# A graph layer on one core: rewritten edge rows and separate own messages against all edges as they lie

## The chip, the cores and the metric

The kernel runs on one core of one Trainium2 chip. The metric is the device time of one execution in microseconds (us), the median of several executions. A run of ten executions of the kernel before gave a median of 17,891.4 us (17,885.6 to 17,897.53).

A core has five engines that each run their own queue of instructions: TensorE (PE, with its weight loads listed as PEld), VectorE (DVE), ScalarE (ACT), GpSimd (POOL) and SyncE (SP). In this kernel SP issues the plain DMAs, and POOL issues the indirect DMAs, that is, the gathers of rows by index.

## The reference

There are 50,000 nodes with 160 numbers each (64 scalars and 32 vectors of 3), and 1,650,000 directed edges with 4 numbers each. The edges come sorted by their target, and every node has one edge to itself among them.

```python
    _loop = jnp.arange(50000, dtype=jnp.int32)
    src = jnp.concatenate([_s, _d, _loop])
    dst = jnp.concatenate([_d, _s, _loop])
    _o = jnp.argsort(dst, stable=True)
...
        m = jnp.concatenate([out0, out1.reshape(-1, 3 * MUL1)], axis=1)
        m_agg = jax.ops.segment_sum(m, dst, num_segments=n)
...
        return x + jax.nn.relu(h)
...
    x = _layernorm(x + _L0_gnn_ref(...), axis=-1)
```

The message `m` of an edge is linear in the source's row `x[src]` and in the edge's four numbers, so the sum over edges can be taken first, of row times edge number, and the weights applied afterwards to each node's sum. Then come a second linear map, relu, the residual and a layer norm. The output is 50,000 x 160 in float32.

## The kernel before

**Groups.** 128 edges make a unit, 6 units (`G`) make a group of 768 edges. A group's targets lie within 32 neighbouring nodes (`W`). For each unit POOL gathers 128 rows of `x` with one indirect DMA (`gather`, L370): 128 rows of 640 B. DVE builds a matrix that has an edge's four numbers in the columns of its target (`spread`, L379 `hot`, L382 `ha`). PE multiplies the two (`group_sums`, L407), six units summed in PSUM. DVE transposes the result (`turn_sums`, L419) and adds it into a ring in SBUF, at a place that is read from a register (L428).

**Tiles.** Two groups (`PG = 2`, a "pair") share one tile of gathered rows `xg`, of 12 gathers. There are 4 buffers of `xg` (pool `rows`), and 2 of the PSUM tile `ps`. The loop at L893 writes out the order by hand for SP, PE, DVE and ACT: in pair p, PE's products run; behind the first of them DVE turns the sums of pair p-1; behind the third, DVE spreads pair p+1. POOL's queue isn't part of that written order and holds nearly nothing but gathers. A gather waits for the landing of an earlier gather that used the same semaphore (there are eight, 110 to 117), and the first gather of a pair also waits for PE's semaphore (118), for the last reader of the buffer it overwrites.

**Supersteps.** 20 groups (`SG`) are loaded and placed at once (`load`, `cast`, `place`, L253 to L364).

**Blocks.** When no later group can touch 128 neighbouring nodes, these are a block: 10 products (`block`, L728, 5 matmuls in two passes), then relu, residual and norm (`norm1` to `norm3`, L184 to L198), one block at a time, and one output DMA for two blocks. All this is handed out between the gathers' products by `after_pair` and `work`.

**Rewritten rows.** After the first 100 groups (`HEAD`), edges are not taken as they lie. `pack` (L486 to L650) reads 790 edges into each of 128 partitions, finds the edges that go from a node to itself, closes the gaps with predicated copies (L582 to L591), and SP writes each row to DRAM (`edges`) at an address from a register (`store`, `put`, L640). The numbers of the removed edges go to `selves`. Supersteps after the first 100 groups load from `edges`. So the removed edges are not gathered.

**Own messages.** The removed edges' part is added densely: for two blocks at once SP reads the nodes' rows four times and their numbers once (`ask_own`, L700 and L705), DVE multiplies (L711 to L713) and transposes them into the ring (L717), in place of part of the zeroing at L675 (`set_own`, `begin_segment`).

This leaves 2,087 groups, that is 12,522 gathers. At the end a flag decides whether a slow second pass (L957 on) is needed.

Of the kernel before, what the change touches and what calls it, by code (L numbers as in the profile page):

```python
# [67 lines left out]
PG = 2  # L68
SG = 20

HEAD = 100
BP = 2
SB = 4
RP = 128
RS = 16
KM = 31
REST = 15
LEAD = 3

def plan(n_nodes, n_edges):  # L80

    nblk = 125
    assert n_nodes % nblk == 0
    assert W == FB
    nb = n_nodes // nblk
    again = 9

    per_unit = P * n_nodes / n_edges
    group = max(g for g in range(1, 17)
                if g == 1 or (g + 0.2) * per_unit + 1 + 5 * math.sqrt(g * per_unit * per_unit / P) <= W)  # L90
    head = math.ceil(min(HEAD, n_edges / (group * P)) / SG) * SG
    eh = head * group * P
    row = group * P + math.floor(per_unit * group * (1 - n_nodes / n_edges))
    assert row * n_nodes / n_edges + 5 * math.sqrt(row * n_nodes / n_edges / 16) < KM

    far = math.ceil(6 * math.sqrt(n_edges) / 2 * n_nodes / n_edges) + 2
    rows = math.ceil((n_edges - eh) / row) + 2
    ngroups = math.ceil((n_edges - n_nodes + eh * n_nodes / n_edges + far) / (group * P))
    assert eh + (rows - 1) * row - n_nodes + eh * n_nodes / n_edges - far >= ngroups * group * P
    units = P * math.ceil(max(math.ceil(n_edges / P) + again - 1, math.ceil((eh + rows * row + 1) / P)) / P)  # L100
    return nblk, nb, again, group, units, ngroups, row, head, rows, far
# [3 lines left out]
def tile_gnn_resnorm(ctx: ExitStack, tc: tile.TileContext, x, src, dst, attr, W1, W2, W3, W4, W5, Ws, Wv, out, n_edges):  # L105
    nc = tc.nc
    N = x.shape[0]
    NBLK, NB, GA, G, NU, NG, L, NH, NR, FAR = plan(N, n_edges)
    EH = NH * G * P
# [71 lines left out]
    def norm1(pool, ph, xt, n):  # L181

        y = pool.tile([P, D], F32, name="y")
        nc.vector.scalar_tensor_tensor(y[:n], ph, 0.0, xt, op0=ALU.max, op1=ALU.add)  # L184
        st = pool.tile([P, 6], F32, name="st")
        nc.vector.bn_stats(st[:n], y[:n])  # L186
        mv = pool.tile([P, 2], F32, name="mv")
        nc.vector.bn_aggr(mv[:n], st[:n])  # L188
        return y, mv

    def norm2(pool, mv, n):
        rstd = pool.tile([P, 1], F32, name="rstd")
        nc.scalar.activation(rstd[:n], mv[:n, 1:2], AF.Sqrt, bias=eps_t[:n])  # L193
        return rstd

    def norm3(o, y, mv, rstd, n):
        nc.vector.reciprocal(rstd[:n], rstd[:n])
        nc.vector.tensor_scalar(o[:n], y[:n], mv[:n, 0:1], rstd[:n], op0=ALU.subtract, op1=ALU.mult)  # L198
        return o
# [4 lines left out]
    def near(g):  # L204
        p = g * G * P
        return p / degree if p <= EH else EH / degree + (p - EH) / (degree - 1)

    nblocks = math.ceil(N / P)
    S = SB * P
    cuts = sorted({0, NH, NG} | {round(i * NG / 10 / SG) * SG for i in range(10)})  # L210
    parts = list(zip(cuts, cuts[1:]))
    offs = []
    for g0, g1 in parts:
        t = min((near(g) / N for g in range(g0, g1 + 1)), key=lambda t: abs(t - 0.5))
        offs.append(math.ceil(5 * math.sqrt(n_edges * max(0, t * (1 - t))) / (degree - 1) + 10))
# [13 lines left out]
    with tc.tile_pool(name="once", bufs=1) as once, tc.tile_pool(name="raw", bufs=2) as rawp, \  # L229
            tc.tile_pool(name="idx", bufs=2) as idxp, tc.tile_pool(name="rows", bufs=4) as rowp, \  # L230
            tc.tile_pool(name="ops", bufs=3) as op, tc.tile_pool(name="sums", bufs=3) as sump, \
            tc.tile_pool(name="ring", bufs=2) as ringp, tc.tile_pool(name="node", bufs=3) as np_, \
            tc.tile_pool(name="ahead", bufs=4) as aheadp, tc.tile_pool(name="outs", bufs=3) as outp, \
            tc.tile_pool(name="psC", bufs=1, space=PSUM) as psC, tc.tile_pool(name="psK", bufs=2, space=PSUM) as psK, \
            tc.tile_pool(name="psP", bufs=1, space=PSUM) as psP, tc.tile_pool(name="psA", bufs=2, space=PSUM) as psA, \
            tc.tile_pool(name="psM", bufs=2, space=PSUM) as psM, ExitStack() as later_pools:

        spotp, ownp = (later_pools.enter_context(tc.tile_pool(name=name, bufs=bufs))
                       for name, bufs in (("spot", 3), ("own", 2)))
# [8 lines left out]
        shareP, sumP = bank[:, 3, 64:64 + NK], bank[:, 3, 96:96 + BP * P // W]  # L248
# [4 lines left out]
        def load(s):  # L253
# [3 lines left out]
            u0, f0 = (g0 * G, g0) if s + 1 < NSC else ((g0 + ng) * G - P, g0 + ng - W)  # L257
# [13 lines left out]
            if g0 >= NH:  # L271
                C = 2 + NK
                if s * SG > NH:
                    f0 = g0 + ng - W
                    at = (at[0], g0 - f0, ng)
                p0, q0 = u0 * P - EH, f0 * G * P - EH
                r6 = rawp.tile([P, NK, W, C], F32, name="r6")
                fd = rawp.tile([P, 1], F32, name="fd")
                fetch_first(fd, edges[0, q0 * C + 1:(q0 + W * G * P) * C + 1], C)
                fetch(r6.rearrange("p b e c -> p b (e c)"), edges[0, p0 * C:(p0 + P * P) * C], C)  # L280
                return s, at, None, None, fd, r6[:, :, :, 0:2].rearrange("p b e c -> p c b e"), r6[:, :, :, 2:]
# [8 lines left out]
            return s, at, ri, fi, None, None, ra  # L290

        def cast(loaded):
            s, at, ri, fi, fd, ef, af = loaded
            if ri is not None:
                ef = rawp.tile([P, 2, NK, W], F32, name="rf")
                fd = rawp.tile([P, 1], F32, name="ff")
                nc.scalar.copy(fd, fi)
                begun.append(nc.scalar.copy(ef, ri))
            return s, at, fd, ef, af
# [23 lines left out]
        def find(g):  # L323

            if g not in spot_of:
                s, u = g // SG, g % SG
                n = min(SG // 2, NG - g)
# [67 lines left out]
        def wrote(kind, ins):  # L395
            ws = written[kind]
            for old in ws[-3] if len(ws) > 2 else []:
                tc.declare_no_dep(ins.ins, old, reason="its reader has waited for it")
# [31 lines left out]
        halves = ((0, L // 2), (L // 2, L))  # L430
        C = 2 + NK
        npacks = math.ceil(NR / RP)
        real = math.ceil((n_edges - EH) / L)
        LW = math.ceil(L / W) * W

        def row_start(r):

            lo, hi = (math.floor(r * L * (1 - 1 / degree)) - 2 * FAR - 2, math.ceil(r * L * (1 - 1 / degree)) + 2 * FAR + 2)
            return (max(lo, 0), hi if r else 0), (max(math.floor((EH + r * L) / degree) - FAR - 2, 0),
                                                  math.ceil((EH + r * L) / degree) + FAR + 2)  # L440

        edges = dram.tile([1, (row_start(NR - 1)[0][1] + L) * C], F32, name="edges")
        selves = dram.tile([1, (row_start(NR - 1)[1][1] + W) * NK], F32, name="selves")
        edge_bytes = edges.bitcast(U8).rearrange("o f -> (o f)")
        self_bytes = selves.bitcast(U8).rearrange("o f -> (o f)")
        rows_stored = [0]

        def row_table(tmp):

            NT = npacks * RP  # L450
            raw = tmp.tile([1, NT], I32, name="raw")
            at = tmp.tile([1, NT], F32, name="at")
            node = tmp.tile([1, NT], F32, name="node")
            nc.vector.memset(raw[:, NR:], 0)
            with nc.allow_non_contiguous_dma(reason="one number of each row"):
                dq.dma_start(raw[:, :NR], dst[EH:EH + NR * L].rearrange("(o r e) -> o r e", o=1, e=L)[:, :, 0])

            nz = math.ceil((row_start(0)[1][1] + W) / P)
            zeros = tmp.tile([P, nz * NK], F32, name="zeros")
            nc.vector.memset(zeros, 0.0)  # L460
            dq.dma_start(selves[0, 0:P * nz * NK].rearrange("(p f) -> p f", p=P), zeros)
            nc.gpsimd.iota(at, pattern=[[L, NT]], base=0, channel_multiplier=0, allow_small_or_imprecise_dtypes=True)
            most, least = math.ceil(EH / degree) + FAR, max(math.floor(EH / degree) - FAR, 0)
            nc.vector.tensor_scalar(node, raw, float(N), float(-most), op0=ALU.min, op1=ALU.add)
            nc.vector.scalar_tensor_tensor(node, at, 1 / degree, node, op0=ALU.mult, op1=ALU.min)
            nc.vector.tensor_scalar(node, node, float(most - least), None, op0=ALU.add)
            nc.vector.scalar_tensor_tensor(node, at, 1 / degree, node, op0=ALU.mult, op1=ALU.max)
            nc.vector.tensor_scalar(node, node, float(least), None, op0=ALU.add)

            nc.vector.tensor_copy(spots[:, :NT], node)  # L470
            nc.vector.tensor_copy(node, spots[:, :NT])

            nc.vector.scalar_tensor_tensor(at, at, node[:, 0:1], node, op0=ALU.add, op1=ALU.subtract)

            moved = raw.bitcast(F32)
            nc.vector.scalar_tensor_tensor(moved[:, :NR], raw[:, :NR], float(N), node[:, :NR],
# [9 lines left out]
        def pack(c, follow):  # L486
# [77 lines left out]
            def close():  # L564
# [5 lines left out]
                if f:  # L570
                    nc.vector.tensor_copy(counts[:f, 1, c:c + 1], cum[:f, L:L + 1])
# [526 lines left out]
```

## Time and profile before

| What | Value |
|---|---|
| median of ten executions | 17,891.4 us |
| the profiled execution: its own time | 17,902.41 us |
| the profiled execution: its span | 17,900.7 us |
| gathers, first and last start | 12,522, 12.1 us and 17,869.0 us |
| PE products of groups (L407) | 25,044, 6,572.0 us |
| DVE `ha` (L382), `hot` (L379) | 1,044 each, 1,830.4 and 572.4 us |
| SP DMAs at L640 (row stores) | 4,236, the last at 16,740.7 us |
| mean granted clock of TensorE | 0.62 |

The span is from the first to the last instruction of one profiled execution. Busy times don't add up to it, because engines work side by side. In the groups, "idle before" is the time in which an engine did nothing just before such an instruction, with what ended it. Lines are lines of the kernel before.

### The profile page before, as it was taken

How to read it: one execution, taken by the hardware profiler on the slowest of the kernel's cores; microseconds unless marked ns; L12 is line 12 of the kernel's file. 1: busy time of each engine (PE TensorE's matmuls, PEld its weight loads, DVE VectorE, ACT ScalarE, POOL GpSimd, SP SyncE). 2: the span in 40 equal slices, each digit the busy share in tenths (PEclk: the TensorE clock that was granted, in tenths of full speed). 3: DMA queues.
4: the chain of work that ended last, by engine and by line, in shares of the span. 5: the costliest groups of instructions: out<-in, count | busy, mean ns of one | idle time of the engine just before them, and what ended most of it. 6: DMA issues, size and time to landing. Idle time of an engine off the chain costs nothing.

```text
span 17900.7 us, 99696 instructions
## 1 busy us (share of the span) xinstructions
PE 7069.9 (39%) x28971; PEld 6135.2 (34%) x28972; DVE 7269.6 (41%) x12244; ACT 226.6 (1%) x484; POOL 11883.8 (66%) x12535
## 2 busy tenths in 40 slices
PE   3334334334343333333434334343334433344334
PEld 3333333333333333333333333333333333333333
DVE  5343534335353342534435244343444434334333
ACT  0000000000000000000000000000000000000000
POOL 6666666666666666666666666666666666666666
PEclk6666666666666666666666666666666666666666
DMA  2222232222222222232222222222222222222222
GB/s 77 74 77 75 77 79 69 79 73 77 77 70 79 75 77 77 70 81 72 78 75 75 77 73 78 74 77 75 72 79 75 77 77 70 77 74 71 75 73 61
DMA packets 862904, 1342.39 MB, mean 75 GB/s; under 512 B 272883, under 2 KB 629752, under 8 KB 858364
## 3 DMA queue, kind: packets, MB, share of 16 engines
q0 software_dynamic: 601056, 1026.60, 21.9%
q1 hardware_dynamic: 259856, 308.09, 6.4%
q8 instruction: 231, 3.78, 0.1%
q14 instruction: 321, 2.63, 0.0%
q10 hardware_dynamic: 1440, 1.29, 0.0%
HBM read 1263.67 MB, written 71.40 MB: 75 GB/s over the span
## 4 chain that ended last, share of the span: by engine, by line
issue 35%; POOL 32%; PE 15%; another core or an unknown queue 6%; DMA 3%; DVE 1%; DVEq 0%; POOLq 0%
POOL xg L370 32%; PE ps L407 13%; DMA xg<-in_x,si 3%; PE phb L728 1%; DVE ha L382 0%; DVE ring L428 0%; DVE pra L589 0%; DVE sums L419 0%; DVE hot L379 0%; DVE ring L717 0%; DVEq L328 0%; DVE pri L584 0%; DVE marks L582 0%; DVE hit L586 0%
## 5 line engine op out<-in xcount | busy, mean ns | idle before, releaser
L370 POOL DMA_INDIRECT xg<-in_x,si x12522 | 11880.1, 949 | 5985.5 <-issue 3660.5
L407 PE MATMUL ps<-xg,ha 128*128 128x160 f32 x25044 | 6572.0, 395 | 10446.5 <-issue 9403.9
L407 PEld LDWEIGHTS ps<-xg,ha 128*128 128x128 f32 x25044 | 5433.8, 263 | 11370.8 <-issue 10385.4
L419 DVE STREAM_TRANSPOSE sums<-ps 128x320 f32<-128x320 f32 x1044 | 527.3, 505 | 5217.3 <-remote 3011.5
L184 DVE SCALAR_TENSOR_TENSOR y<-phb,xt 128x160 f32<-128x160 f32 x391 | 125.9, 322 | 4802.8 <-PE ps L407 3116.3
L382 DVE TENSOR_TENSOR ha<-hot,pk 128x1536 f32<-128x1536 f32 x1044 | 1830.4, 1753 | 39.2 <-DVE hot L379 2.1
L728 PE MATMUL phb<-BWk,ring 128*128 128x160 f32 (+1 forms) x3910 | 1174.7, 388 | 323.6 <-issue 323.2
L728 PEld LDWEIGHTS phb<-BWk,ring 128*128 128x128 f32 (+1 forms) x3910 | 928.9, 267 | 331.6 <-issue 330.9
L428 DVE TENSOR_TENSOR ring<-ring,sums 128x160 f32 x2087 | 684.6, 328 | 295.6 <-issue 205.2
L379 DVE TENSOR_TENSOR hot<-bank,rel 128x384 f32<-128x384 f32 x1044 | 572.4, 548 | 0.0
L717 DVE STREAM_TRANSPOSE ring<-xr 128x1280 f32<-128x1280 f32 x188 | 465.2, 2475 | 6.5
L589 DVE COPY_PREDICATED prow<-marks,prow 128x2370 f32<-128x2370 int32 (+8 forms) x160 | 445.7, 2786 | 1.1
L193 ACT ACTIVATE rstd<-mv,eps_t 128x1 f32<-128x1 f32 x391 | 115.2, 295 | 17255.3 <-DVE mv L188 5659.4
L589 DVE COPY_PREDICATED pra<-marks,pra 128x1580 f32<-128x1580 int32 (+8 forms) x160 | 305.8, 1911 | 0.0
L713 DVE TENSOR_TENSOR xr<-xr,bank 128x1280 f32<-128x1280 f32 x188 | 278.9, 1483 | 6.7 <-issue 0.4
L198 DVE TENSOR_SCALAR o<-y,mv,rstd 128x160 f32<-128x160 f32 x391 | 148.1, 379 | 21.2 <-remote 5.0
L425 DVE TENSOR_TENSOR ring<-ring 128x196 f32<-128x196 f32 (+20 forms) x485 | 149.2, 373 | 1.8
L186 DVE BATCH_NORM_STATS2 st<-y 128x6 f32<-128x160 f32 x391 | 128.2, 328 | 13.4
L675 DVE MEMSET ring<- 128x1280 f32 (+1 forms) x98 | 119.3, 1218 | 22.9 <-issue 22.9
L586 DVE COPY_PREDICATED_SCALAR hit<-marks,none 128x395 int32 (+8 forms) x160 | 105.2, 657 | 5.7
L352 DVE STREAM_TRANSPOSE pk<-r 128x512 f32<-128x512 f32 x100 | 104.5, 1045 | 0.0
L587 DVE COPY_PREDICATED hit<-marks,pri 128x395 int32<-128x395 int32 (+8 forms) x160 | 95.6, 598 | 6.2 <-issue 0.7
(343 smaller groups left out, 1681.2 us busy)
## 6 DMA issues: line engine op xcount, KB each, us to landing
xg<-in_x,si POOLq DMA_INDIRECT x12522
xr<-in_x SPq DMA_DIRECT2D x748, 160.0 KB
r<-edges SPq DMA_DIRECT2D x100, 384.0 KB
edges<-prow SPq DMA_DIRECT2D x1994, 18.5 KB
selves<-mine SPq DMA_DIRECT2D x1992, 0.5 KB
xt<-in_x SPq DMA_DIRECT2D x195, 160.0 KB
out<-o SPq DMA_DIRECT2D x195, 160.0 KB
pra<-in_attr SPq DMA_DIRECT2D x15, 1580.0 KB
```

Source lines behind the costliest of these rows:

```text
L198: nc.vector.tensor_scalar(o[:n], y[:n], mv[:n, 0:1], rstd[:n], op0=ALU.subtract, op1=ALU.mult)
L370: nc.gpsimd.indirect_dma_start(out=xg[:, j, :], out_offset=None, in_=x, in_offset=bass.IndirectOffsetOnAxis(ap=placed[0][:, u + j:u + j + ...
L379: nc.vector.tensor_tensor(hot[:, :n], slotsP[:, 0:W].unsqueeze(1).to_broadcast([P, n, W]), rel[:, u:u + n].unsqueeze(2).to_broadcast([P, n ...
L382: nc.vector.tensor_tensor(ha[:, :n], hot[:, :n].unsqueeze(2).to_broadcast([P, n, NK, W]), pk[:, :, u:u + n].rearrange("p k u -> p u k").un ...
L407: mm = nc.tensor.matmul(ps[:, j // G, :], ha[:, j].rearrange("p k w -> p (k w)"), xr, start=j % G == 0, stop=j % G == G - 1)
L419: nc.vector.transpose(at[:, :ng], ps[:, :ng].rearrange("p g (b f) -> p g b f", f=FB))
L425: nc.vector.tensor_tensor(ring[k][:, b, :past], ring[k][:, b, :past], ring[k - 1][:, b, S:S + past], op=ALU.add)
L428: nc.vector.tensor_tensor(here, here, at[:, i], op=ALU.add)
L589: nc.vector.copy_predicated(what[:n, a:e], mi[:, r].unsqueeze(2).to_broadcast([n, e - a, what.shape[2]]), what[:n, a + d:e + d])
L713: nc.vector.tensor_tensor(xr[:, :nq], xr[:, :nq], sumP[:, :nq].unsqueeze(2).to_broadcast([P, nq, D]), op=ALU.mult)
L717: nc.vector.transpose(ring[k][:, :, c0:c0 + nq * W].rearrange("p b (w q) -> p q b w", q=nq), xr[:, :nq].rearrange("p q (b f) -> p q b f", ...
L728: wrote("misc", nc.tensor.matmul(ph[:nb], ring[k][:, i, c0:c0 + nb], BWk[:, i, :], start=i == 0, stop=i == ND - 1))
```

## The change

All edges are taken from the inputs as they lie. `pack`, its DRAM tables, `row_table`, `store` and the checks that belong to them go. `ask_own` and `set_own` go, and the ring is zeroed in full. An edge from a node to itself is gathered like any other. The number of groups becomes `ceil(1,650,000 / 768) = 2,149`, which is 12,894 gathers.

Three groups share a tile (`PG = 3`: 18 gathers to a tile) and a superstep has 21 groups. The pools change: 5 buffers of `xg` in place of 4, 3 of `ps` in place of 2, 2 of `sums` in place of 3, 3 of `xt` in place of 4, 2 of `o` in place of 3. The norms of two blocks share their instructions where the operation allows it. The delays of the handed-out work are cut, in tiles, since a tile is longer.

```diff
-PG = 2
-SG = 20
-HEAD = 100
+PG = 3
+SG = 21
...
-LEAD = 3
+LEAD = 2
...
+    ngroups = math.ceil(n_edges / (group * P))
...
-            tc.tile_pool(name="idx", bufs=2) as idxp, tc.tile_pool(name="rows", bufs=4) as rowp, \
-            tc.tile_pool(name="ops", bufs=3) as op, tc.tile_pool(name="sums", bufs=3) as sump, \
+            tc.tile_pool(name="idx", bufs=2) as idxp, tc.tile_pool(name="rows", bufs=5) as rowp, \
+            tc.tile_pool(name="ops", bufs=3) as op, tc.tile_pool(name="sums", bufs=2) as sump, \
...
-            tc.tile_pool(name="psP", bufs=1, space=PSUM) as psP, tc.tile_pool(name="psA", bufs=2, space=PSUM) as psA, \
+            tc.tile_pool(name="psA", bufs=3, space=PSUM) as psA, \
...
-            if g0 >= NH:
...
-                fetch(r6.rearrange("p b e c -> p b (e c)"), edges[0, p0 * C:(p0 + P * P) * C], C)
...
             ring[k] = ringp.tile([P, ND, TW], F32, name="ring")
-            own = own_blocks(k)
-            end = min((own[-1][-1] + 1) * P, nblocks * P) - k * S if own else 0
-            nc.vector.memset(ring[k][:, :, end:], 0.0)
+            for b in range(ND):
+                nc.vector.memset(ring[k][:, b], 0.0)
...
+            if b == bs[-1]:
+                resid[b] = norm1(np_, sums_of.pop(bs[0])[:nb, :m], of_nodes.pop(bs[0])[:nb, :m], nb, m)
...
-            after_pair(max(p - 3, START), begin_segment, k)
-            for bs in own_blocks(k):
-                got = []
-                for part in range(NK):
-                    after_pair(p - 8 + part, ask_own, k, bs, got, part)
-                after_pair(p - 2, set_own, k, bs, got)
+            after_pair(max(p - 2, START), begin_segment, k)
...
-            for d, f in ((2, do_block), (3, do_root), (4, do_store), (6, do_send)):
+            for d, f in ((1, do_block), (2, do_root), (3, do_store), (4, do_send)):
                 after_pair(p + d, f, b)
...
-                if packs and p >= START:
-                    when = p + (j + 1) / (ng * G)
...
-                    for step in packs[0][done:todo]:
```

## The prediction

> **What bounds the kernel now.** I read the page's busy times and its chain of what ended last, then POOL's waits, then POOL's timeline across a few stalls, then tables of windows cut exactly from one stall's end to the next.
>
> ```profile
> span 17900.7 us, 99696 instructions
> PE 7069.9 (39%) x28971; PEld 6135.2 (34%) x28972; DVE 7269.6 (41%) x12244; ACT 226.6 (1%) x484; POOL 11883.8 (66%) x12535
> issue 35%; POOL 32%; PE 15%; another core or an unknown queue 6%; DMA 3%; DVE 1%; DVEq 0%; POOLq 0%
> ```
>
> No engine is full. POOL is the busiest with 66%, and the chain runs mostly through its gathers and the "issue" time between them.
>
> ```profile
> POOL xg L370 <- issue: 3660.5, 11946, 2.7
> POOL xg L370 <- PE ps L407: 1537.4, 289, 12.0
> POOL xg L370 <- remote: 686.0, 175, 7.0
> POOL xg L370 <- PE phb L728: 59.4, 11, 6.6
> ```
>
> POOL's waits (total us, times, longest): a gather takes 0.95 us and 0.30 us of "issue" lie before the next; and 289 + 175 + 11 = 475 times POOL stands still, 2,282.8 us in all, 4.81 us each.
>
> ```profile
> 17243.87 0.95 POOL L370 DMA_INDIRECT xg<-in_x,si  x1 [0.30 <-issue]
> 17245.12 0.94 POOL L370 DMA_INDIRECT xg<-in_x,si  x1 [0.30 <-issue]
> 17252.30 0.94 POOL L370 DMA_INDIRECT xg<-in_x,si  x1 [6.24 <-PE ps L407]
> 17253.55 0.98 POOL L370 DMA_INDIRECT xg<-in_x,si  x1 [0.31 <-issue]
> ```
>
> In POOL's timeline a gather starts every 1.25 us until a tile's first gather waits some 6 us for PE's semaphore. One would say that PE is late, and that more buffers help. The windows say otherwise. Each begins where a stall ends; columns are PE, PEld, DVE, ACT and POOL busy with instruction counts.
>
> ```profile
> 16945.80:16977.60 31.80, 12.25 (x61) 11.03 (x60) 7.47 (x14) 0.30 (x1) 22.68 (x24) 0.66 0.23 62
> 16977.60:16996.80 19.20, 6.84 (x20) 5.60 (x21) 3.83 (x8) 0.00 (x0) 11.35 (x12) 0.50 0.25 68
> 17098.90:17150.10 51.20, 20.21 (x84) 17.57 (x83) 16.36 (x42) 0.29 (x1) 34.04 (x36) 0.63 0.22 58
> 17150.10:17201.20 51.10, 21.54 (x92) 18.41 (x91) 11.80 (x23) 0.59 (x2) 34.30 (x36) 0.60 0.31 79
> 17252.20:17286.60 34.40, 14.27 (x64) 13.44 (x62) 20.27 (x40) 0.29 (x1) 22.77 (x24) 0.65 0.45 107
> ```
>
> 36 gathers take 51.1 to 51.2 us, whether DVE runs 42 instructions or 23 and PE 84 products or 92: 1.42 us each. 24 gathers take 34.4 us: 1.43 each, with a stall that is shorter in proportion. And where a stall ended early (24 gathers in 31.8), the next took what was missing (12 in 19.2): together 36 in 51.0. Something with a fixed pace of 1.42 us for a gather stands behind POOL; POOL runs ahead of it at 1.25 until the buffers are full, then waits for it. The trace doesn't name it. It isn't PE's count of products or DVE's work, by these rows.
>
> ```profile
> 236.70:698.90 462.20, 182.98 (x743) 160.68 (x742) 202.91 (x323) 4.23 (x16) 306.53 (x324) 0.62 0.26 72
> 877.10:16210.40 15333.30, 6076.27 (x24856) 5277.37 (x24856) 6286.25 (x10512) 191.65 (x405) 10191.67 (x10752) 0.62 0.29 76
> 17098.90:17832.30 733.40, 286.80 (x1195) 245.04 (x1194) 225.98 (x453) 4.71 (x16) 489.40 (x516) 0.61 0.26 68
> ```
>
> Three long windows give the pace with different neighbours. At 236.7 to 698.9, edges come as they lie (the first 600 gathers), `pack` works, and there are no own messages (the first `xr` load is at 728.4): 462.2 / 324 = 1.4265. In the long middle there is everything: 15,333.3 / 10,752 = 1.4261. After the last row store (16,740.7) `pack` is over and own messages go on: 733.4 / 516 = 1.4213.
>
> **The change part by part.** *More gathers.* 2,149 groups in place of 2,087: 12,894 gathers, 372 more. At POOL's own 1.25 us they cost 465 us, at the pace of 1.42 us 529 us.
>
> *`pack` goes.* Its DVE instructions (L448 to L613) sum to 1,946 us and its 4,236 row stores fill SP's queue. All of it lies beside the gathers: with it the pace is 1.4261, without it 1.4213. So it is worth 0.0048 us a gather, 61 us.
>
> *Own messages go, and loads come from the inputs.* DVE's L690 to L720 sum to 831 us, SP's `xr` and `sa` loads are 943 DMAs; a superstep now has four loads and two small ACT casts. The pace with own messages and rewritten rows (1.4261) and without either (1.4265) is the same, so I take nothing. Bounds: half of DVE's remaining load may be worth another 0.0048 (pace 1.4165), or the gain without `pack` may not show (1.4261).
>
> *Zeroing the ring, spreads, norms.* All on DVE, none on the path. A full zeroing is 3.26 us (the 128x3840 form of L675) x 98 = 319 us, against 119 now. `ha` took 1.75 us for 1,536 columns and 0.95 for 768, so 0.15 + 1.046 per thousand columns: 2.56 us for 2,304, x 717 tiles = 1,833, as now (1,830). Joined norms save at most half of their 539 us. DVE ends near 7,270 - 1,946 - 831 + 200 = 4,700 us, a quarter of the span. What covers it is the gap between its tiles, 25.6 us for 18 gathers; if that cover went, 2.6 us a tile x 717 = 1,860 us would be the price, but nothing brings it near.
>
> *What waits now.* A tile's first gather still waits for PE's last reader, five tiles back; behind it in POOL's queue stand only gathers. PE's first product of a tile waits for DVE's `ha`, written one tile ahead, and for a `ps` buffer, of which there are three. SP loses nearly all its queue, so loads and outputs aren't late. Deeper buffers (90 gathers against 48) let POOL run further ahead and stall less often and longer; by the windows that changes no pace.
>
> *Ends.* The first 600 gathers took 877.1 us, 21.4 more than 600 x 1.4261; I keep that (bounds 0, since part of it falls at the first own messages, and 21.4). The last gather started 31.7 us before the end; with tiles half as long again up to 47.6.
>
> The sum for the span: 21.4 + 12,893 x 1.4213 + 31.7 = 18,378 us. The span shown is 9.3 us above the median of 17,891.4, so the median should be **18,369 us**, 2.7% slower. The same sum for the kernel before, with 12,521 x 1.4261, gives 17,909 against a span of 17,900.7.
>
> *A rule that speaks against this.* POOL's gathers took 940 to 3,260 ns, mean 949, so all that lies above the shortest is 11,880.1 - 12,522 x 0.940 = 109 us; with DVE at 41% (middle) or 31% (last window) the pace moved 0.3%. The Trainium skill (SBUF — State Buffer, section "SBUF: two separate sides") says that a DVE instruction in a two-port mode locks GpSimd out, so that it can't write a gather's descriptors. By that rule alone, taking 2,777 us of work from DVE could free up to as much of POOL's time, and the kernel would end near 15,600 us. The rows leave at most 109 us for it, and the sum above goes by the rows.
>
> **The rivals.** *A, the stalls belong to the buffers (faster).* If a stall has a price of its own, 90 gathers of buffer in place of 48 make stalls rarer. Without stalls a gather takes (11,880.1 + 5,985.5 - 475 x 4.51) / 12,522 = 1.256 us, with 4.51 = 4.81 less the ordinary 0.30 and 5,985.5 POOL's whole idle time before gathers. Then 12,894 x 1.256 = 16,192; stalls come every 26.4 x 90/48 = 49.4 gathers, 261 x 4.51 = 1,177; with 12.1 at the start and 31.7 at the end 17,413, a median of 17,404. It wins as soon as stalls cost under 0.129 us a gather ((17,900.7 - 43.8 - 16,192) / 12,894), against 0.171 now. For it: the stalls are put down to PE. Against: 24 and 36 gathers cost the same each, and a short stall is paid back.
>
> *B, the pace belongs to the tile (faster).* Every full tile of before has 12 gathers, so a fixed part for a tile can't be told from one for a gather. At most it is 12 x (1.421 - 1.256) = 1.99 us; then 716 tiles of 18 take 24.59 us each, 17,615, with the ends (43.8) and 9.3 off a median of 17,650. Against: a fixed part would be a handshake of PE and DVE, and their counts moved nothing in the windows.
>
> *C, slower than forecast.* One stretch ran slower: the 24 gathers from 698.9 to 740.6 took 41.7 us in place of 34.2. If something of that kind came in one of 50 tiles, 14 x 7.5 = 108 us more: 18,477.
>
> *D, the change doesn't do what it says:* a group that reaches over 32 nodes would set the flag and run the slow second pass, with a time of another order. The groups hold 768 edges as before, at 33 instead of 32 edges a node, so they span fewer nodes. Under 1%.
>
> **How the numbers follow.** Forecast, 80%: pace 1.4165 to 1.4261, startup 0 to 21.4, end 31.7 to 47.6, thus 18,286 to 18,446. A 7%, B 4%, something between B and the forecast 4%, C 4%, D under 1%. The forecast's own range leaves out 20%; I widen it by 36 us below, for a fixed part of 0.05 us in each of 717 tiles: 18,250 to 18,446. A measurement of this kernel can tell about 0.2% from no change. Faster by more than that: A, B and a quarter of the between, 12%; within 0.2%: 1%, of the between; slower: the rest, 87%.
>
> **What would show it.** Right: windows between stall ends give 1.415 to 1.426 us a gather; stalls come at multiples of 18 gathers, at intervals of 54 or 72, each 8 to 13 us long, at some 200 in number; DVE's busy time falls to 4,500 to 5,000 us with no gain from it. Wrong: stalls that stay at 4 to 7 us while intervals grow (A), a pace of 1.36 to 1.40 (B), gathers whose mean falls below 0.94 us, or POOL waiting for DVE.

## The result and the profile after

| | Kernel before | Changed kernel |
|---|---|---|
| median | 17,891.27 us (17,883.65 to 17,899.37, 28 executions) | 18,771.61 us (18,756.36 to 18,805.23, 8 executions) |
| ratio | 1 | 1.0493, interval 1.0484 to 1.0502 |
| span of the profiled execution | 17,900.7 us | 18,764.9 us |
| stops: gathers that start over 1.8 us after the one before | 467 | 330 |

The change makes the kernel 4.9% slower, 880 us. The forecast was 2.7%, 18,369 us: 403 us are missing. The page of the changed kernel, its span, its busy times and its chain:

```profile
span 18764.9 us, 87300 instructions
PE 7179.6 (38%) x29715; PEld 5939.9 (32%) x29716; DVE 4710.1 (25%) x8412; ACT 100.8 (1%) x405; POOL 12263.8 (65%) x12904
issue 11%; POOL 10%; PE 4%; another core or an unknown queue 1%; DMA 1%; DVE 0%; DVEq 0%; POOLq 0%
```

DVE has 2,559 us less to do, and the program 12,396 instructions fewer, and neither shortened anything. The chain's shares add up to some 27% of the span, so it says little here. POOL's waits say more (total us, times, longest):

```profile
POOL xg L346 <- issue: 4230.0, 12481, 15.3
POOL xg L346 <- PE ps L384: 1793.8, 238, 17.6
POOL xg L346 <- remote: 333.6, 82, 9.1
POOL xg L346 <- PE phb L435: 60.8, 9, 8.8
```

The longest "issue" was 2.7 us before and is 15.3 us now, and the longest wait put down to PE rose from 12.0 to 17.6 us. Something new stops POOL, and a part of it is put down to nothing at all. Windows from one stop's end to the next, with the columns of the prediction's windows, find it:

```profile
10167.60:10218.85 51.25, 22.42 (x102) 18.83 (x102) 11.45 (x20) 0.68 (x3) 34.13 (x36) 0.63 0.28 72
10218.85:10269.85 51.00, 19.70 (x89) 16.20 (x89) 17.71 (x38) 0.29 (x1) 34.30 (x36) 0.63 0.21 58
10371.80:10433.00 61.20, 29.99 (x133) 26.74 (x134) 19.77 (x41) 0.30 (x1) 34.15 (x36) 0.60 0.22 58
10872.90:10949.60 76.70, 26.45 (x114) 22.36 (x113) 17.73 (x29) 0.68 (x3) 51.61 (x54) 0.59 0.22 58
```

36 gathers still take 51.0 to 51.3 us and 54 take 76.7: the pace of before. But the third window takes 61.2 us for 36 gathers. It ends at gather 7,182, which is 57 x 126: the first gather of a superstep (7 tiles of 18). I sorted all stops by the place of the gather in its superstep:

| Stops of the changed kernel | Number | Pace of the intervals that they end | Median stop, from start to start |
|---|---|---|---|
| before a multiple of 126 | 55 | 1.640 us per gather | 14.4 us |
| all others | 274 | 1.418 us per gather | 7.2 us |

The 55 intervals hold 1,962 gathers; (1.640 - 1.418) x 1,962 = 436 us. That is the missing time and a little more, an upper estimate of what these stops cost. The timeline of the stop before gather 7,182 shows what happens in it (start, duration, engine, line, operation; in brackets the idle time before):

```profile
10414.50 0.95 POOL L346 DMA_INDIRECT xg<-in_x,si  x1 [0.30 <-issue]
10415.75 0.94 POOL L346 DMA_INDIRECT xg<-in_x,si  x1 [0.31 <-issue]
...
10422.79 10.93 PE L384 MATMUL ps<-xg,ha 128*128 128x160 f32 x62 [0.28 <-issue]
...
10423.02 0.68 DVE L396 STREAM_TRANSPOSE sums<-ps 128x480 f32<-128x480 f32 x1 [39.54 <-PE phb L435]
10423.74 1.04 DVE L405 TENSOR_TENSOR ring<-ring,sums 128x160 f32 x3
...
10425.48 2.56 DVE L358 TENSOR_TENSOR ha<-hot,pk 128x2304 f32<-128x2304 f32 x1
...
10431.08 1.06 DVE L328 STREAM_TRANSPOSE pk<-ra 128x512 f32<-128x512 f32 x1
10432.06 0.25 DVE L331 TENSOR_SCALAR si<-bank 128x126 int32<-128x126 f32 x1
...
10433.08 0.95 POOL L346 DMA_INDIRECT xg<-in_x,si  x1 [16.38 <-PE ps L384]
```

DVE's transpose at 10423.02 starts when PE's signal (its semaphore) tells that the third tile (tile 2, counted from 0) of the superstep is done, and by the same signal the buffer for the first tile of the next superstep comes free. At the usual 7.2 us after the last gather (10415.75) POOL could go on at 10422.95. It doesn't: the gather's indices `si` are written only at 10432.06, at the end of what DVE does in the next tile (turned sums, spread, a block's norm, the placing), and the gather starts 1.0 us later. The profile names PE for this wait, though PE's signal had come 10 us before. The writer of the gather's other operand ended last. This holds for all 55: each of these gathers starts 0.77 us after the end of the instruction that writes its `si`. In the trace of the kernel before none of the 49 that stop at a superstep's first gather does; there `si` was written over 9 us earlier.

**The rule behind it.** A superstep has T tiles, counted from 0, and there are B buffers of gathered rows. The first gather of the next superstep, tile T, finds its buffer free when tile T - B is done. The placing of the next superstep is done in tile q. The gather waits for the placing if q is larger than T - B.

| Kernel | T - B | q |
|---|---|---|
| before | 10 - 4 = 6 | 5 |
| changed | 7 - 5 = 2 | 3 |

So the kernel before had a pair to spare, and the changed one is a tile short. The rule is read from the code; the experiments test it.

### The profile page after: what moved, and what is told of

Read it like the earlier page. It is cut to its first block, busy times and chain, and to the rows that moved or that the text cites. A ratio compares the mean times of both kernels' runs of the same rounds, so it can differ in the third digit from the quotient of the medians.

```text
span 18764.9 us, 87300 instructions
## 1 busy us (share of the span) xinstructions
PE 7179.6 (38%) x29715; PEld 5939.9 (32%) x29716; DVE 4710.1 (25%) x8412; ACT 100.8 (1%) x405; POOL 12263.8 (65%) x12904
## 5 line engine op out<-in xcount | busy, mean ns | idle before, releaser
L346 POOL DMA_INDIRECT xg<-in_x,si x12894 | 12262.7, 951 | 6453.9 <-issue 4230.0
L384 PE MATMUL ps<-xg,ha 128*128 128x160 f32 x25788 | 6448.0, 371 | 10004.8 <-issue 9369.7
L384 PEld LDWEIGHTS ps<-xg,ha 128*128 128x128 f32 x25788 | 5184.2, 242 | 11137.8 <-issue 10449.1
L396 DVE STREAM_TRANSPOSE sums<-ps 128x480 f32<-128x480 f32 x717 | 483.2, 674 | 11955.9 <-PE ps L384 8627.9
L358 DVE TENSOR_TENSOR ha<-hot,pk 128x2304 f32<-128x2304 f32 x717 | 1829.6, 2552 | 24.6
L355 DVE TENSOR_TENSOR hot<-bank,rel 128x576 f32<-128x576 f32 x717 | 536.8, 749 | 0.1
L170 DVE SCALAR_TENSOR_TENSOR y<-phb,xt 128x320 f32<-128x320 f32 x196 | 95.6, 488 | 1484.9 <-PE ps L384 939.3
L429 DVE MEMSET ring<- 128x747 f32 x490 | 333.7, 681 | 51.2
L402 DVE TENSOR_TENSOR ring<-ring 128x235 f32<-128x235 f32 (+6 forms) x485 | 147.4, 370 | 2.2
L328 DVE STREAM_TRANSPOSE pk<-ra 128x512 f32<-128x512 f32 x103 | 108.3, 1052 | 4.3 <-DMA ra<-in_attr 4.3
```

Source lines behind the costliest of these rows:

```text
L328: begun.append(nc.vector.transpose(pk.rearrange("p k (l b) -> p k b l", b=NK), af.rearrange("p b e k -> p k b e")))
L346: nc.gpsimd.indirect_dma_start(out=xg[:, j, :], out_offset=None, in_=x, in_offset=bass.IndirectOffsetOnAxis(ap=placed[0][:, u + j:u + j + ...
L355: nc.vector.tensor_tensor(hot[:, :n], slotsP[:, 0:W].unsqueeze(1).to_broadcast([P, n, W]), rel[:, u:u + n].unsqueeze(2).to_broadcast([P, n ...
L358: nc.vector.tensor_tensor(ha[:, :n], hot[:, :n].unsqueeze(2).to_broadcast([P, n, NK, W]), pk[:, :, u:u + n].rearrange("p k u -> p u k").un ...
L384: mm = nc.tensor.matmul(ps[:, j // G, :], ha[:, j].rearrange("p k w -> p (k w)"), xr, start=j % G == 0, stop=j % G == G - 1)
L396: nc.vector.transpose(at[:, :ng], ps[:, :ng].rearrange("p g (b f) -> p g b f", f=FB))
```

## Experiments

**Theory S:** the 400 us are this wait for `si`. **Rival T:** they come with the longer tile. **Rival L:** they come with the loads, which arrive in shorter pieces. Two edits take the wait away from the changed kernel, one adds it to the kernel before, and one has all edges as they lie in the old tiles of two groups. Ratios are to the kernel before on the same chip, since chips differ, as the first four showed.

`place_early`, the placing one tile earlier (q = 2):

```diff
-                after_pair(p + 1, do_cast, s + 1)
-                after_pair(p + 2, do_place, s + 1)
+                after_pair(p, do_cast, s + 1)
+                after_pair(p + 1, do_place, s + 1)
```

> The changed kernel with the casts and the placing of the next superstep handed out one tile earlier (casts in tile 1 of 7, placing in tile 2 in place of 3); nothing else differs. Theory S (the loss over the forecast is POOL's wait, at the first gather of a superstep, for the indices that the placing writes; with 5 buffers of 7 tiles, POOL gets there when DVE is at tile 2): the long stalls of 14 to 17 us at multiples of 126 gathers vanish, the pace falls from 1.452 to about 1.42 us a gather, time 18,290 to 18,450 us. Theory L (loads of the edges as they lie, in short pieces, slow the gathers) and theory T (the larger tile has a price in each tile): no change, 18,770 us.

`rows4`, four buffers (T - B = 3):

```diff
-            tc.tile_pool(name="rows", bufs=5) as rowp
+            tc.tile_pool(name="rows", bufs=4) as rowp
```

> The changed kernel with 4 buffers of gathered rows in place of 5. Theory S: POOL then stops for its buffer one tile earlier, and the placing is done by the time it asks for the indices; fewer buffers make the kernel faster, 18,290 to 18,450 us. Theories L and T: 18,770 us. If buffers as such are worth something: over 18,800 us.

`pairs`, the changed kernel with the tiles, buffers and delays of before:

```diff
-PG = 3
-SG = 21
+PG = 2
+SG = 20
...
-                after_pair(p + 2, do_place, s + 1)
+                after_pair(p + 4, do_place, s + 1)
```

> All edges as they lie and no own messages, as in the changed kernel, but with the tiles of before: two groups to a tile, 20 groups to a superstep, 4 buffers of rows, 2 of the sums in PSUM, and the delays of before (placing in pair 5 of 10). Theory S: no wait for the indices, 18,300 to 18,450 us. Theory L: 18,700 to 18,800 us. Theory T: 18,300 to 18,450 us, so this run with place_early tells S from T.

`before_place_late`, the kernel before with q = 7:

```diff
-                after_pair(p + 4, do_place, s + 1)
+                after_pair(p + 6, do_place, s + 1)
...
-                    after_pair(p + 5, examine_all)
+                    after_pair(p + 7, examine_all)
```

> The kernel before with the placing of the next superstep handed out two pairs later (pair 7 of 10 in place of 5; the final check moves with it). With 4 buffers POOL asks for the next superstep's indices when DVE is at pair 6. Theory S: a wait of some 4 us comes at most of the 104 superstep starts, 18,200 to 18,350 us. Theories L and T: no change, 17,890 us.

**Measured: nothing that tells.** On this chip the kernel before took 15,751.77 us, not 17,891. `place_early` took 16,171.83, `rows4` 16,172.89, `pairs` 16,173.46 (ratios 1.0266, 1.0266, 1.0267, interval 1.0249 to 1.0284), `before_place_late` 15,753.97 (1.0, 0.999 to 1.001). POOL doesn't run into its buffers there, so a wait on `si` can't show.

**The same on a second chip, with the changed kernel as a control, and with a third of the products left out:**

> The changed kernel as it is, as a control, since the kernel before took 17,891 us on the chip of the result and 15,752 us on the chip of the first four experiments, where POOL never stopped. All theories: where the kernel before takes about 17,890 us, 18,770 us with stalls of 14 to 17 us at multiples of 126 gathers; where it takes about 15,752 us, 16,172 us and no stall over 2 us, since there POOL never runs more than a few gathers ahead of TensorE.

> The changed kernel with the cast and the placing of the next superstep handed over one tile earlier. Where the kernel before takes about 17,890 us: theory S (the first gather of a superstep waits for its placed indices) 18,290 to 18,450 us, and no stall longer than 13 us at multiples of 126 gathers; theory T (the price comes with the longer tile or the loads, not with the placing) 18,770 us. Where it takes about 15,752 us: both 16,172 us, and the run tells nothing.

> The kernel before with its placing two pairs later, so that the first gather of a superstep meets the placing only after its buffer is free. Where the kernel before takes about 17,890 us: theory S 18,200 to 18,350 us, with longer stalls at multiples of 120 gathers; theory T 17,890 us. Where it takes about 15,752 us: both the same time as before.

```diff
             for j, xr in enumerate(rows):
+                if j % G in (2, 4):
+                    yield ps
+                    continue
                 mm = nc.tensor.matmul(ps[:, j // G, :], ha[:, j].rearrange("p k w -> p (k w)"), xr,
```

> The changed kernel with a third of the products left out (the third and the fifth of each group of six), so that its output is not the reference's; every gather, the DVE work and the waits between tiles stay. Theory P: the pace of 1.42 us per gather is that of TensorE's instructions, which come one product (two loads and two matmuls) per 1.40 us while POOL gathers, and POOL's stalls are TensorE catching up; then, where the kernel before takes about 17,890 us, POOL's stalls go and the pace is 1.25 us, 16,170 us in all. Rival Q: POOL's stalls are its own (its queue, or the transfers), and 18,770 us stay, or 18,370 us if only the wait at the superstep goes. Where the kernel before takes about 15,752 us POOL is the bound in any case: 16,170 us by both.

Again a chip without stops: before 15,750.39 us, control 16,195.41 (ratio 1.0283, 1.0266 to 1.03), `place_early2` 16,194.81, `before_place_late2` 15,752.55, `thin_pe` 16,197.28. POOL's waits in the control:

```profile
POOL xg L346 <- issue: 3704.6, 12162, 0.3
POOL xg L346 <- PE ps L384: 208.7, 685, 0.3
```

No wait of a gather for PE is longer than 0.3 us. PE follows each gather as it lands:

```profile
10001.06 0.94 POOL L346 DMA_INDIRECT xg<-in_x,si  x1 [0.30 <-issue]
10001.12 0.50 PEld L384 LDWEIGHTS ps<-xg,ha 128*128 128x128 f32 x2 [0.68 <-DMA xg<-in_x,si]
10001.12 0.90 PE L384 MATMUL ps<-xg,ha 128*128 128x160 f32 x2 [0.28 <-DMA xg<-in_x,si]
```

Here the change costs 445 us, the price of its 372 gathers at 1.253 us (466) less some 20. The late placing costs nothing where POOL isn't far ahead.

**A slowed TensorE, so that POOL runs ahead on any chip.** `slow_pe` is the changed kernel with

```diff
+                for again in range(5 if j % G == 0 else 1):
...
-                                      start=j % G == 0, stop=j % G == G - 1)
+                                          start=j % G == 0, stop=j % G == G - 1 or (j % G == 0 and again < 4))
```

and `slow_pe_early` the same with the early placing; `place_early3` is `place_early` once more.

> The changed kernel with the first product of each group of six done five times over (each time afresh, so the sums stay the same): ten products for six rows, so that TensorE falls behind POOL on any chip and POOL runs five tiles ahead, as it does on the chip of the result. TensorE becomes the bound: ten products of 0.86 to 1.05 us for six gathers, 18,400 to 22,600 us in all. Theory S: POOL is stopped at every tile until TensorE's last reader of the buffer; before the first gather of a superstep (multiples of 126) it is stopped longer, since its indices are placed only in the tile after, about 7 to 10 us later than the buffer is free; the next stop is shorter by as much, and the time is TensorE's. Rival T: the stops at multiples of 126 are like those at other multiples of 18.

> The same with the cast and the placing handed over one tile earlier. Theory S: the stops at multiples of 126 are like those at other multiples of 18, and the time is that of slow_pe within 0.5%, since TensorE sets it. Rival T: the two kernels stop alike.

> The changed kernel with the cast and the placing handed over one tile earlier, once more, to meet a chip on which the kernel before takes 17,890 us. There theory S says 18,290 to 18,450 us and theory T 18,770 us; where the kernel before takes about 15,750 us both say 16,170 to 16,200 us.

The third chip has the stops: before 17,980.29 us; one execution of each kernel. `place_early3` took 18,444.85, as S said, but had no control beside it. `slow_pe` took 20,029.66 and `slow_pe_early` 19,729.03. The stops at multiples of 126 have a median of 12.7 us (96 of them, a tenth over 21 us) with the late placing and 4.9 us (74) with the early one; most of the others lie between 4.5 and 13.5 us in both. S had said that the early ones would be like the others; in length they are shorter, since fewer gathers lie before them. By pace they are alike: intervals that end at a multiple of 126 take 1.52 us per gather with the early placing and the others 1.53, against 1.80 and 1.50 with the late one. That speaks for S. That the times would agree within 0.5% was wrong: they differ by 1.5%. TensorE, slowed to ten products for six rows, still didn't set the time alone.

**The decisive set, with a control, on a fourth chip that has the stops:**

> The changed kernel as it is, as a control beside the next three. Where the kernel before takes 17,890 to 17,980 us: 18,770 to 18,860 us, ratio 1.049, POOL stopped some 14 us at about 55 multiples of 126 gathers and some 7 us elsewhere. Where it takes 15,750 us: 16,170 to 16,200 us and no stop.

> The cast and the placing one tile earlier. Where POOL stops: theory S ratio 1.022 to 1.031 to the kernel before, 2% under the control, and stops of some 7 us at multiples of 126 as elsewhere; theory T the control's time. Where it does not: the control's time by both.

> The kernel before with its placing two pairs later. Where POOL stops: theory S 1.5 to 2.5% over the kernel before, with the added time in the stops at multiples of 120 gathers (14 us in place of 5.5); theory T no difference. Where it does not: no difference by both.

| On this chip | Median | Ratio | Stops at the superstep's first gather |
|---|---|---|---|
| before | 17,982.37 us | 1 | not profiled here; 49, median 5.5 us, on the result's chip |
| `after_ctl2`, the changed kernel | 19,048.23 us | 1.059 (1.0572 to 1.0607) | 84, median 16.1 us |
| `place_early4` | 18,468.79 us | 1.0271 (1.0253 to 1.0288) | 58, median 7.5 us |
| `before_place_late3` | 18,498.03 us | 1.0289 (1.0272 to 1.0306) | 88, median 11.0 us |

S holds in both directions: two changed lines take 579 us from the changed kernel, and two others add 516 us to the kernel before, which keeps its rewritten rows, own messages, loads and tiles. T and L would have left both alone. The sizes were forecast less well: the control is 5.9% over the kernel before, not 4.9%, with 84 long stops in place of 55; the early placing is worth 3.0%, not 2%; and the late one costs 2.9% (1.5 to 2.5% expected), with stops of 11.0 us (14 expected). Why this chip has more of the long stops than the result's was not looked into. `pairs` was not run on a chip with stops. In `place_early4`, around gather 5,796 = 46 x 126:

```profile
8276.65 0.94 POOL L346 DMA_INDIRECT xg<-in_x,si  x1 [0.30 <-issue]
...
8283.97 0.68 DVE L396 STREAM_TRANSPOSE sums<-ps 128x480 f32<-128x480 f32 x1 [36.27 <-remote]
...
8284.21 0.95 POOL L346 DMA_INDIRECT xg<-in_x,si  x1 [6.61 <-remote]
```

The gather now starts 0.24 us after DVE's transpose, in place of 10.06 us. Of the 58 gathers with such a stop, 6 still start 0.77 us after `si`: with q equal to T - B there is nothing to spare. The first waits of POOL in `place_early4`, and then in `before_place_late3`:

```profile
POOL xg L346 <- issue: 3804.9, 12478, 0.6
POOL xg L346 <- PE ps L384: 1849.4, 278, 16.9
```

```profile
POOL xg L370 <- issue: 4422.4, 12029, 32.7
POOL xg L370 <- PE ps L407: 1127.6, 182, 14.6
```

The long "issue" is gone with the early placing (0.6 us, against 15.7 in the control beside it) and appears in the kernel before with the late one (32.7 us, against 2.7).

**What the ordinary stops are.** `thin_pe2` is `thin_pe` on the same chip:

> The changed kernel with a third of the products left out (output not the reference's), all gathers kept. Where POOL stops: theory P (the stops are TensorE catching up, since it gets through about one product per 1.4 us while POOL gathers) 16,170 to 16,400 us, POOL hardly stopped, 1.25 us per gather; rival Q (the stops are POOL's own or the transfers') 18,300 to 18,770 us with stops as in the control. Where POOL does not stop: 16,170 to 16,200 us by both.

It took 19,049.22 us (one execution), the control's time. P falls; Q's stops stay, though its range, made for the result's chip, was missed. An ordinary window of it:

```profile
13003.61:13105.24 101.63, 28.71 (x109) 22.55 (x108) 16.61 (x28) 0.30 (x1) 68.24 (x72) 0.57 0.24 63
```

72 gathers in 101.6 us are 1.41 us each, with a third fewer products. Stops are rarer and longer: 12.5 us from start to start after 72 gathers, where `place_early4` has 7.3 after 36. Less the usual 1.25 that is 0.156 and 0.168 us per gather, as if each gather left a debt.

The transfers are not what POOL waits for: in the result's trace the last DMA packet of the gathers ends at most 2.9 us after the start of the last gather before a stop, and the stop goes on: some 5 us more in the median of the ordinary stops and 12 us in that of the long ones.

`pool_rest` tells a debt from a wait for the tile. It is `place_early` with

```diff
             for j in range(n):
+                if j % 6 == 0:
+                    nc.gpsimd.memset(xg[:, j:j + 6, :], 0.0)
                 nc.gpsimd.indirect_dma_start(
```

> The kernel with the early placing, and before every six gathers POOL clears their six rows of the tile first: 2,149 clears of 128x960 on POOL, by its IOTA of 128x790 (792 ns) an estimate of 0.96 us each, 2,060 us in all. Theory R: on a chip where POOL stops, a stop is a debt of 0.16 us per gather that is worked off whenever POOL issues no gather; the clears take the place of the stops, and the time stays at 18,450 us within 1.5%. Rival B2: the stops belong to TensorE's pace or to the tile, and the clears only delay the gathers: 18,450 + 2,060 = 20,510 us, with stops of some 7 us as before. Where POOL does not stop: 16,175 + 2,060 = 18,240 us by both.

> The changed kernel with four buffers of gathered rows in place of five, its placing as late as in the change. Where POOL stops: theory S 1.022 to 1.031 of the kernel before (18,380 to 18,540 us where that takes 17,982), since the buffer of a superstep's first tile is now free one tile later, when the placing is done; theory T, or a loss by fewer buffers, 19,050 us or more. Where it does not: 16,170 to 16,200 us by all.

Both ran on the chip of the decisive set, one execution each, the kernel before at 17,891.06 us this time. `rows4_2` took 18,379.02 us, 2.7% over it, with 49 stops of median 7.3 us at multiples of 126: S once more, and 10 us over the prediction's 18,369. `pool_rest` took 18,518.36 us. POOL's groups in it:

```profile
L348 POOL DMA_INDIRECT xg<-in_x,si x12894 | 12249.1, 950 | 3792.2 <-issue 3703.3 <-POOL xg L347 53.3 <-DMA xg<-in_x,si 24.9
L347 POOL MEMSET xg<- 128x960 f32 x2149 | 1890.4, 915 | 543.2 <-PE ps L386 304.3 <-remote 225.1 <-PE phb L437 13.4
```

1,890 us of clears cost 139 us beside `rows4_2`, the nearest run of that day (`place_early` itself was not run beside it). In the trace they come two at a time, after every twelve gathers. They stand where POOL stood still: what is left of waiting before a tile is 543 us, against some 2,280 us in `rows4_2` (1,930.7 + 268.3 + 84.3 of POOL's waits). B2 falls. The times alone leave another rival: something that takes 1.42 us per gather whatever POOL does, beside which the clears would cost as little. The trace speaks for the debt: averaged over 1,072 such stretches, 1.1 matmuls per us start on PE as a pair of clears begins, 2.5 per us in its fourth us, and 1.1 again before the next pair. So on these chips a gather seems to leave 0.16 us of something that gets done when POOL issues no gather, and stops are where it gets done. What it is no run shows; the last section has what the traces tell of it.

No version beat the kernel before on a chip with stops or without: the best of the changed ones, `rows4` and `place_early`, are 2.6 to 2.8% over it on both kinds.

## Why the prediction was right and wrong, point by point

- **The direction and the price of 372 more gathers: right.** Without the new wait the change costs what the forecast said, 1.027: 1.0271 (`place_early4`), 18,379 us (`rows4_2`).
- **The pace of 1.4213 us per gather: right, on chips of this kind.** Ordinary intervals of the changed kernel run at 1.4176, 48 us less over 12,893 gathers. On the chips with stops the pace stayed at 1.41 to 1.43 whatever the tile, the buffers, DVE's work or a third fewer products; only `slow_pe` and `slow_pe_early`, with ten products for six rows, moved it, to 1.50 and 1.53. On the chips without stops the same kernels run at 1.25, which the prediction couldn't know. It was worked out from a chip with stops and met one: on the other kind its 18,369 us would have been some 13% too high.
- **"What waits now": the failed step.** It said that a tile's first gather waits for PE's last reader five tiles back. It named one operand of the gather, the buffer, and not the other, `si`. It also said that deeper buffers change no pace: true of the pace, but with them POOL reaches a superstep's first gather before its indices exist. The term that was left out is 436 us in the result's trace (55 intervals). That sum runs high: in `after_ctl2` it gives 715 us, where the early placing took off 579. T - B = 2 and q = 3 could have been read from the code beforehand, and DVE's 10 us from rows of its tile. At most 102 supersteps x 10 us = 1,020 us, an estimate, would have been a bound to keep.
- **The ends: as bounded.** The last gather started 47.6 us before the end (31.7 taken, up to 47.6), and the first 600 gathers took 868.5 us (877.1 before).
- **Nothing for own messages, loads, zeroing, spreads and norms: right.** `ha` took 2.552 us (2.56 said), DVE 4,710.1 us (4,700 said), all of it hidden. The forecast's 831 us for own messages and 539 us for norms include 16 and 6 us of semaphore instructions, so the work was 814 and 533 us; nothing hung on it. But DVE's 10 us behind a tile's end are not hidden from a gather that needs `si`; the cover of 25.6 us a tile that the prediction named was counted for PE's `ha` alone.
- **The rule that two-port DVE work locks GpSimd out** (the Trainium skill, SBUF — State Buffer, "SBUF: two separate sides"): DVE lost 2,559 us and a gather's mean went from 949 to 951 ns. No gain by it shows, as the bound of 109 us had it. Whether any of that work ran in such a mode the traces don't tell.
- **Rivals.** A and B (faster) fell with the pace. C (slower) had the right side and a wrong mechanism: a stretch of 7.5 us in one of 50 tiles, where the true one was 7.9 us (436 / 55) in 55 of 717. D did not happen.
- **Signs.** Stops at multiples of 18: right. Intervals of 54 or 72, 8 to 13 us for a stop and some 200 stops: wrong, mostly 36 (228 of 329), 7.2 us and 330 stops. "POOL waiting for DVE", a sign of being wrong, came true, though the profile's list of waits puts it down to PE and "issue". Five buffers didn't make POOL stop less often than every second tile.

The terms, against the forecast span of 18,378 us: pace -48, wait for `si` +436, end +16, start -3.5 (868.5 - 600 x 1.4176 = 17.9 in place of 21.4), together about 18,779; the span was 18,764.9.

## What to carry to other kernels

When tiles, buffers or hand-over delays change together, redo for each operand of the leading engine's first instruction when it is written and when the engine may first want it: here tiles per superstep less buffers must not be smaller than the tile that does the placing. A deeper buffer helps only while everything else that the engine needs is as far ahead. A wait that the profile puts down to an engine long done, or to "issue" with a new and long maximum, is another operand's: look in the timeline for what was written last before the wait ended.

## What the runs showed of the hardware that was not expected

- **Chips differ by some 14% on this kernel.** The kernel before took 15,750.39 and 15,751.77 us on two chips and 17,891 to 17,982 us on others (one chip gave 17,982.37 and later 17,891.06). A gather takes 947 to 951 ns in the traces of both kinds; on the first POOL doesn't stop for its buffers, on the second it does, by some 0.16 us per gather. TensorE's mean granted clock doesn't explain it, since it was lower on the faster chips: 0.56 to 0.57 in the runs of the kernel before, against 0.62 on the slower ones.
- **On the chips with stops, PE falls behind while POOL gathers.** From the timeline of the changed kernel in the result's trace:

```profile
10408.79 0.29 PEld L384 LDWEIGHTS ps<-xg,ha 128*128 128x128 f32 x1 [2.51 <-issue]
10411.59 0.29 PEld L435 LDWEIGHTS phb<-BWk,ring 128*128 128x128 f32 x1 [2.51 <-issue]
10414.39 0.29 PEld L435 LDWEIGHTS phb<-BWk,ring 128*128 128x128 f32 x1 [2.51 <-issue]
```

The loads start 2.80 us apart, with a matmul halfway between them, so one instruction comes per 1.40 us (not a whole product, as the expectation of `thin_pe` has it), and no wait explains the idle time. That holds only late in a run of gathers: averaged over the result's trace, 3.2 to 5.2 matmuls per us start in the first 12 us after POOL resumes, and 0.3 to 0.6 per us from 22 us on. In the long stop shown above, 62 matmuls, or 31 products, pass in 10.93 us, but only from 10422.79 on, 6 us after POOL's last gather ended. Leaving out a third of the products didn't change the pace, so this shows that PE is held up, not that its work is the bound.

- **On these chips PE's signal comes long after its matmuls.** All 25,788 matmuls of the changed kernel's groups are in the trace, 36 to a tile. The row below holds the last eight of tile 2 of the long stop's superstep; the very last starts at 10386.70. DVE's transpose, which waits for it, starts at 10423.02, 36 us later.

```profile
10385.75 1.58 PE L384 MATMUL ps<-xg,ha 128*128 128x160 f32 x10
```

Over 716 tiles of the result's trace the distance is 7.5 us in the median and over 36.9 us in a quarter of them; on the chip without stops (`after_ctl`) the median is 0.51 us. So at an ordinary stop POOL waits for a signal whose matmul started long before. Why the signal is late, and why one chip does this and another doesn't, was not tried.
